# Gathering rows of x and normalising them in place while the table of h is made (24 of 131 groups), with h kept transposed in DRAM and whole blocks of rows to a partition

## The chip, the cores and the metric

The kernel runs on one core of a Trainium2 chip. The metric is the device time of one execution in microseconds (us). The median of three runs of the kernel before is 2666.79 us (2663.8 to 2667.16). The profile and the trace come from another, profiled execution of the same kernel. Lower is better.

## The reference

The kernel computes one layer of a graph network on 12,500 nodes of 256 features, with 200,000 edges sorted by destination:

```python
h = maximum(layernorm(x, axis=-1), 0)
agg = segment_sum(h[src], dst, num_segments=N)
z = (1 + eps_gin) * h + agg
t = relu(batchnorm(z @ W1 + b1, g1, bt1))           # 256 -> 512, statistics over the nodes
out = x + relu(batchnorm(t @ W2 + b2 + h, g2, bt2)) # 512 -> 256
```

All is float32. The index `src` is random, so `h[src]` is a gather of 200,000 rows of 1 KB; each batchnorm needs all nodes before the next step can begin.

## The kernel before

**Indices.** The edges are cut into 1563 tiles of 128 edges, and 12 tiles make a group: 131 groups. src and dst are brought into `srcT` and `dstT`, one column a tile. A `flag` tells whether the destinations are spread evenly enough for the fast form; a branch on it (If and Else, at the end of the program's text) chooses `fast()` or `general()`. Here it is `fast()`.

**The table (lines 257 to 295).** For each of 25 chunks of 512 nodes, rows of x are loaded to `xt`, normalised (per row on DVE BN_STATS and BN_AGGR, square root and the final scaling with relu on ACT), and stored to `h_tab` in DRAM. A partition holds four consecutive rows, so a piece of a transfer is 4 KB (`move`). TensorE transposes the chunk, and DVE and ACT copy it with a stride into `hT`, the transposed h, which stays in SBUF to the end.

**The gather stage (lines 318 to 420).** `gather(i)` issues 12 indirect DMAs on POOL's queue, each of which fetches 128 rows of `h_tab` into a slice of a buffer `gt`. `sums(i)` builds on DVE the 0/1 matrices `oh` (which edge goes to which of 128 local destinations), multiplies them with the gathered rows on TensorE (12 matmuls into one `ps`), copies `ps` to `zs` on ACT, and builds `at`, which places local destinations in a window of 280 nodes. `put(i)` multiplies `zs` with `at` (two matmuls, `pz`) and adds the result to the chunk `zc` on DVE; `zc` begins as hT times 1 + eps on ACT. As soon as a chunk is complete, `first_layer` multiplies it with W1 (16 passes, `ph`), takes statistics on DVE, copies to `ts` on ACT, and stores `t_tab` in DRAM.

A float32 matmul shows as two passes in the profile. The loop issues `gather(i + AHEAD)`, then `sums(i)`, then `put(i - 1)`. With AHEAD = 2 there are three buffers `gt`, so a gather waits until TensorE is done with the group three before. The order of the instructions on each engine is made by a scheduler from the program's text; each engine works through its own list in order, and waits by semaphores: a row that waits holds all that stand behind it.

**Second layer and last pass (lines 425 to 474).** For each chunk `ti` is loaded from t_tab, scaled with relu on ACT (`tT`), multiplied with W2 (`py`), and hT is added in place. After the second statistics, ACT makes `yr` (reading hT with a stride), TensorE transposes back (`po`), DVE adds rows of x (`xr`), and `out` is stored from ACT's queue.

Of the kernel before, what the change touches and what calls it, by code (L numbers as in the profile page):

```python
# [19 lines left out]
AHEAD = 2  # L20
# [8 lines left out]
def kernel(  # L29
# [24 lines left out]
    assert N % R == 0  # L54
# [208 lines left out]
    def fast():  # L263
        with ExitStack() as fs:
            keep = fs.enter_context(tc.tile_pool(name="keep", bufs=1))
            t_tab = dram.tile([NCH, P, HC, CH], F32, name="t_tab")

            hT = [keep.tile([P, DC, w * R], F32, name=f"hT{g}") for g, (_, w) in enumerate(chunks)]


            with tc.tile_pool(name="ln", bufs=3) as ln, tc.tile_pool(
                name="ps_h", bufs=2, space=PSUM
            ) as ps_h:
                for g in range(NCH):
                    n0, w = chunks[g]
                    n = w * R
                    xt = ln.tile([P, R, D], F32, name="xt", bufs=4)
                    move(nc.sync, xt, x, g, store=False)
                    ht = ln.tile([P, R, D], F32, name="ht")
                    layernorm(ln, xt, w, ht)  # L280
                    move(nc.sync, ht, h_tab, g, store=True)
                    pz = ps_h.tile([P, DC, CH], F32, name="pz")
                    for d in range(DC):
                        for c in range(R):
                            nc.tensor.transpose(  # L285
                                pz[:, d, c * w : (c + 1) * w], ht[:w, c, d * P : (d + 1) * P],
                                ident[:w, :w],
                            )
                        side = hT[g][:, d, :].rearrange("p (w c) -> p c w", c=R)
                        came = pz[:, d, :n].rearrange("p (c w) -> p c w", c=R)  # L290
                        if d % 2:
                            nc.scalar.copy(side, came)
                        else:
                            nc.vector.tensor_copy(side, came)


            with ExitStack() as es:
                gat = es.enter_context(tc.tile_pool(name="gat", bufs=AHEAD + 1))
                sel = es.enter_context(tc.tile_pool(name="sel", bufs=2))
                zcp = es.enter_context(tc.tile_pool(name="zc", bufs=3))  # L300
                tsp = es.enter_context(tc.tile_pool(name="ts", bufs=2))
                ps_i = es.enter_context(tc.tile_pool(name="ps_i", bufs=1, space=PSUM))
                ps_s = es.enter_context(tc.tile_pool(name="ps_s", bufs=2, space=PSUM))
                ps_z = es.enter_context(tc.tile_pool(name="ps_z", bufs=1, space=PSUM))
                ps_t = es.enter_context(tc.tile_pool(name="ps_t2", bufs=3, space=PSUM))
# [12 lines left out]

                groups = [(t0, min(GT, NTILE - t0)) for t0 in range(0, NTILE, GT)]
                gathered = {}  # L320

                def gather(i):
                    t0, n = groups[i]
                    gs = []
                    ga = gat.tile([P, GT, D], F32, name="gt")
                    for t in reversed(range(t0, t0 + n)):
                        rows = left if t == full_tiles else P
                        nc.gpsimd.indirect_dma_start(  # L328
                            out=ga[:rows, t - t0, :], out_offset=None, in_=h_tab,
                            in_offset=bass.IndirectOffsetOnAxis(ap=srcT[:rows, t : t + 1], axis=0),  # L330
                        )
                        gs.append((t - t0, rows))
                    gathered[i] = ga, gs
# [3 lines left out]
                def z_chunk(c):  # L337
# [4 lines left out]
                    nc.scalar.activation(zc[c][:, :, :n], hT[c], AF.Copy, scale=gin1)  # L342
# [4 lines left out]
                summed = {}  # L347

                def sums(i):
# [9 lines left out]
                    ga, gs = gathered.pop(i)  # L359
                    ps = ps_s.tile([P, D], F32, name="ps")  # L360
                    for k, (j, rows) in enumerate(gs):
# [362 lines left out]
```

## Time and profile before

| | us |
|---|---|
| median of 3 runs | 2666.79 |
| the profiled execution | 2652.91 |
| its span, first to last instruction | 2651.0 |
| indices, up to the branch | 0 to about 29 |
| table of h | about 29 to 149 |
| gather stage, first to last gather on POOL | 149.1 to 2362.3 |
| its last sums and first layers | 2362 to 2392 |
| second layer | 2392 to 2564 |
| last pass | 2564 to 2651 |

The page names an instruction by line, engine, operation and tiles (out<-in). The engines are PE (TensorE; PEld is its weight load), DVE (VectorE), ACT (ScalarE), POOL (GpSimd) and SP (DMA queues only). In a row of groups stands the busy time, the mean of one in ns, then the idle time of the engine just before and what ended it ("issue": nothing that the profile shows). In a row of waits stands the sum, how often, and the longest. In a timeline a bracket holds the idle time before a row. PEclk is the granted clock of TensorE, 1.00 being full.

### The profile page before, as it was taken

How to read it: one execution, taken by the hardware profiler on the slowest of the kernel's cores; microseconds unless marked ns; L12 is line 12 of the kernel's file. 1: busy time of each engine (PE TensorE's matmuls, PEld its weight loads, DVE VectorE, ACT ScalarE, POOL GpSimd, SP SyncE). 2: the span in 40 equal slices, each digit the busy share in tenths (PEclk: the TensorE clock that was granted, in tenths of full speed). 3: DMA queues.
4: the chain of work that ended last, by engine and by line, in shares of the span. 5: the costliest groups of instructions: out<-in, count | busy, mean ns of one | idle time of the engine just before them, and what ended most of it. 6: DMA issues, size and time to landing. Idle time of an engine off the chain costs nothing.

```text
span 2651.0 us, 14241 instructions
## 1 busy us (share of the span) xinstructions
PE 1623.6 (61%) x4881; PEld 1029.4 (39%) x4881; DVE 633.8 (24%) x1017; ACT 346.8 (13%) x561; POOL 1483.4 (56%) x1575
## 2 busy tenths in 40 slices
PE   3564556755665576556456556666565656569985
PEld 2333344433443343334334334434343334444444
DVE  6611121211221122112112112121121212124443
ACT  4710000000000000000000000000000000004446
POOL 0056667666766666666676676666666676640000
PEclk6566677776776786767777766767776677779985
DMA  5633333333333333333333333333333333325437
GB/s 176 227 101 90 95 101 115 105 95 101 115 105 95 111 105 105 96 111 105 107 97 109 106 98 102 110 105 112 95 105 110 91 114 102 111 78 214 159 130 281
DMA packets 101342, 310.96 MB, mean 117 GB/s; under 512 B 27684, under 2 KB 32362, under 8 KB 95118
## 3 DMA queue, kind: packets, MB, share of 16 engines
q0 software_dynamic: 75008, 204.90, 26.3%
q1 hardware_dynamic: 21744, 91.21, 9.6%
q10 hardware_dynamic: 4510, 13.86, 1.3%
q8 instruction: 41, 0.67, 0.1%
q14 instruction: 39, 0.32, 0.0%
HBM read 258.66 MB, written 51.20 MB: 117 GB/s over the span
## 4 chain that ended last, share of the span: by engine, by line
issue 28%; PE 26%; POOL 25%; another core or an unknown queue 9%; DMA 3%; DVE 2%; ACT 2%; ACTq 0%; POOLq 0%
POOL gt L328 25%; PE ps L362 13%; PE py L441 6%; PE ph L397 4%; DMA gt<-h_tab,srcT 3%; PE pz L380 2%; ACT yr L460 2%; DVE oh L353 1%; PE po L467 1%; DVE zc L389 1%; DVE ot L471 0%; DVE mv L229 0%; DVE at L369 0%; DVE st L401 0%
## 5 line engine op out<-in xcount | busy, mean ns | idle before, releaser
L328 POOL DMA_INDIRECT gt<-h_tab,srcT x1563 | 1481.8, 948 | 850.5 <-issue 458.2
L362 PE MATMUL ps<-gt,oh 128*128 128x256 f32 x3126 | 987.1, 447 | 643.0 <-issue 559.4
L362 PEld LDWEIGHTS ps<-gt,oh 128*128 128x128 f32 x3126 | 672.5, 221 | 949.5 <-issue 738.8
L389 DVE TENSOR_TENSOR zc<-pz,zc 128x560 f32<-128x560 f32 (+9 forms) x203 | 101.0, 527 | 1518.0 <-PE ps L362 863.5
L380 PE MATMUL pz<-at,zs 128*128 128x280 f32 x524 | 194.5, 498 | 181.4 <-DVE zc L389 114.8
L367 ACT COPY zs<-ps 128x256 f32<-128x256 f32 x131 | 48.9, 373 | 1739.4 <-PE ps L362 1147.3
L397 PE MATMUL ph<-zc,w1s 128*128 128x512 f32 (+1 forms) x400 | 197.0, 648 | 80.4 <-DVE zc L389 56.9
L353 DVE TENSOR_TENSOR oh<-col,dstT 128x1536 f32<-128x1536 f32 x131 | 227.8, 1739 | 14.5 <-issue 14.5
L380 PEld LDWEIGHTS pz<-at,zs 128*128 128x128 f32 x524 | 119.5, 237 | 235.0 <-issue 209.2
L441 PE MATMUL py<-tT,w2s 128*128 128x512 f32 (+1 forms) x400 | 169.5, 587 | 4.6 <-ACT tT L434 4.6
L397 PEld LDWEIGHTS ph<-zc,w1s 128*128 128x128 f32 x400 | 82.4, 211 | 181.1 <-issue 117.5
L401 DVE BATCH_NORM_STATS2 st<-ph 128x6 f32<-128x512 f32 (+1 forms) x100 | 68.4, 684 | 265.9 <-remote 93.7
L441 PEld LDWEIGHTS py<-tT,w2s 128*128 128x128 f32 x400 | 76.4, 192 | 97.7 <-issue 86.7
L402 ACT COPY ts<-ph 128x512 f32<-128x512 f32 (+1 forms) x100 | 57.3, 573 | 334.0 <-DVE st L401 251.9
L285 PE MATMUL pz<-ident,ht 128*128 128x128 f32 (+1 forms) x200 | 65.0, 442 | 54.1 <-ACT ht L259 19.5
L434 ACT ACTIVATE tT<-ti,of,sc 128x512 f32<-128x512 f32 (+1 forms) x100 | 72.3, 796 | 91.3 <-issue 86.4
L467 PE MATMUL po<-ident,yr 128*128 128x128 f32 (+1 forms) x200 | 47.6, 413 | 35.6 <-ACT yr L460 35.6
L285 PEld LDWEIGHTS pz<-ident,ht 128*128 128x128 f32 (+1 forms) x200 | 36.6, 205 | 82.5 <-ACT ht L259 40.7
L369 DVE TENSOR_SCALAR at<-col,shift 128x280 f32<-128x280 f32 x131 | 65.5, 500 | 0.0
L460 ACT ACTIVATE yr<-hT,of,sc 128x512 f32<-128x512 f32 (+1 forms) x50 | 59.9, 1276 | 20.1 <-DVE ot L471 19.2
L445 DVE TENSOR_TENSOR hT<-py,hT 128x512 f32<-128x512 f32 (+1 forms) x50 | 33.9, 678 | 100.9 <-PE py L441 100.9
L467 PEld LDWEIGHTS po<-ident,yr 128*128 128x128 f32 (+1 forms) x200 | 37.5, 214 | 45.7 <-ACT yr L460 45.7
(68 smaller groups left out, 307.6 us busy)
## 6 DMA issues: line engine op xcount, KB each, us to landing
gt<-h_tab,srcT POOLq DMA_INDIRECT x1563
t_tab<-ts SPq DMA_DIRECT2D x24, 1024.0 KB
ti<-t_tab SPq DMA_DIRECT2D x24, 1024.0 KB
xt<-in_x_dram SPq DMA_DIRECT2D x24, 512.0 KB
h_tab<-ht SPq DMA_DIRECT2D x24, 512.0 KB
xr<-in_x_dram SPq DMA_DIRECT2D x24, 512.0 KB
out_dram<-ot ACTq DMA_DIRECT2D x24, 512.0 KB
rawi_d<-in_dst_dram SPq DMA_DIRECT2D x1, 768.0 KB
```

What stands on the lines that cost most here:

```text
L285: nc.tensor.transpose(pz[:, d, c * w : (c + 1) * w], ht[:w, c, d * P : (d + 1) * P], ident[:w, :w],)
L328: nc.gpsimd.indirect_dma_start(out=ga[:rows, t - t0, :], out_offset=None, in_=h_tab, in_offset=bass.IndirectOffsetOnAxis(ap=srcT[:rows, t ...
L353: nc.vector.tensor_tensor(oh[:, :n, :], col[:, :P].unsqueeze(1).to_broadcast([P, n, P]), dstT[:, t0 : t0 + n].unsqueeze(2).to_broadcast([P ...
L362: nc.tensor.matmul(ps, lhsT=oh[:rows, j, :], rhs=ga[:rows, j, :], start=(k == 0), stop=(k == n - 1),)
L380: nc.tensor.matmul(pz[:, d, :WIDE], lhsT=zs[:, d * P : (d + 1) * P], rhs=at, start=True, stop=True)
L389: nc.vector.tensor_add(side, pz[:, :, a - lo : b - lo], side)
L397: nc.tensor.matmul(ph[:, :n], lhsT=w1s[:, d, f * P : (f + 1) * P], rhs=zc[c][:, d, :n], start=(d == 0), stop=(d == DC - 1),)
L401: nc.vector.bn_stats(st1[:, f, c, :], ph[:, :n])
L434: nc.scalar.activation(tT[:, f, :n], ti[:, f, :n], AF.Relu, bias=of1[:, f : f + 1], scale=sc1[:, f : f + 1],)
L441: nc.tensor.matmul(py[:, :n], lhsT=w2s[:, f, d * P : (d + 1) * P], rhs=tT[:, f, :n], start=(f == 0), stop=(f == HC - 1),)
L460: nc.scalar.activation(yr[:, d, :, :w], hT[g][:, d, :].rearrange("p (w c) -> p c w", c=R), AF.Relu, bias=of2[:, d : d + 1], scale=sc2[:, d ...
L467: nc.tensor.transpose(po[:w, c, d * P : (d + 1) * P], yr[:, d, c, :w], ident)
```

## The change

- **First groups.** `LEAD` = 24: groups 0 to 23 gather from x itself, not from h_tab. `settle` then normalises the gathered rows in place: six BN_STATS on DVE, each over two rows at once (read alternately, so that the operation's statistics of even and odd elements are those of the two rows), a square root on ACT, two small operations on DVE, and 12 scalings with relu on ACT.
- **The table between them.** There is no table stage. `h_chunk` makes the same 25 chunks within iterations 0 to 19 of the loop: rows normalised by `settle`, stored to h_tab from ACT's queue, transposed through one PSUM bank `pc` (half a chunk at a time), copied to `hc` by DVE or ACT without a stride, and stored to `h_cols`, a new tensor in DRAM that holds h transposed. From group 24 on, gathers read h_tab and wait for its stores.
- **h from DRAM.** `z_chunk` loads zc from h_cols, one chunk ahead, and scales it in place; the second layer loads `yT` from h_cols, after `ti`, and works on it in place of hT.
- **Buffers and order.** AHEAD = 4, so five buffers `gt`; `zc` has four, `ph` two for three. `sums` and `put` are split, so that TensorE's work on `zs` of group i − 1 stands near the beginning of group i's. The 12 matmuls go over the tiles forward, while the gathers are issued backward. t_tab is stored from ACT's queue.
- **Blocks of rows.** `carry` takes the place of `move` in the fast form: partition p takes rows p, 128 + p, 256 + p, 384 + p of a chunk, in pieces of 1 KB. yr is then read and written without a stride, and the last chunk is handled in pieces.
- **Two Ifs** (flag 0, flag 1) for If and Else.

```diff
-AHEAD = 2
+AHEAD = 4
+LEAD = 24
...
+        def carry(eng, sb, table, g, store):
+            n0 = chunks[g][0]
+            for c0, c1, rows in pieces(g):
+                if c0 == c1:
+                    continue
+                side = table[n0 + c0 * P : n0 + (c1 - 1) * P + rows, :].rearrange("(c p) d -> p c d", p=rows)
+                if store:
+                    eng.dma_start(side, sb[:rows, c0:c1, :])
+                else:
+                    eng.dma_start(sb[:rows, c0:c1, :], side)
...
+                def settle(v, pairs, rows, to, tag):
+                    n = 2 * pairs
+                    st = sel.tile([P, n, 3], F32, name="st" + tag)
+                    for c in reversed(range(0, n, 2)):
+                        nc.vector.bn_stats(
+                            st[:, c : c + 2, :].rearrange("p c s -> p (c s)"),
+                            v[:, c : c + 2, :].rearrange("p c d -> p d c"),
+                        )
+                    sd = sel.tile([P, n], F32, name="sd" + tag)
+                    nc.scalar.activation(sd, st[:, :, 2], AF.Sqrt, bias=epst, scale=1.0 / D)
+                    rs = sel.tile([P, n], F32, name="rs" + tag)
+                    nc.vector.reciprocal(rs, sd)
+                    nb = sel.tile([P, n], F32, name="nb" + tag)
+                    nc.vector.scalar_tensor_tensor(nb, st[:, :, 1], -1.0, rs, op0=OP.mult, op1=OP.mult)
+                    for c in reversed(range(rows)):
+                        nc.scalar.activation(
+                            to[:, c, :], v[:, c, :], AF.Relu, bias=nb[:, c : c + 1], scale=rs[:, c : c + 1]
+                        )
...
+                def h_chunk(g):
+                    n = chunks[g][1] * R
+                    slots = len(parts[g])
+                    x_chunk(g + 2)
+                    ht = ln.tile([P, R, D], F32, name="ht")
+                    settle(xts.pop(g), -(-slots // 2), slots, ht, "c")
+                    carry(nc.scalar, ht, h_tab, g, store=True)
+                    hc = ln.tile([P, DC, CH], F32, name="hc")
+                    for d in range(DC):
+                        ph = ps_h.tile([P, CH], F32, name="pc")
+                        for c in range(slots):
+                            nc.tensor.transpose(
+                                ph[:, c * P : (c + 1) * P], ht[:, c, d * P : (d + 1) * P], ident
+                            )
+                        if d % 2:
+                            nc.scalar.copy(hc[:, d, :n], ph[:, :n])
+                        else:
+                            nc.vector.tensor_copy(hc[:, d, :n], ph[:, :n])
+                    nc.sync.dma_start(h_cols[g, :, :, :n], hc[:, :, :n])
...
-                            out=ga[:rows, t - t0, :], out_offset=None, in_=h_tab,
+                            out=ga[:rows, t - t0, :], out_offset=None, in_=x if i < LEAD else h_tab,
...
-                    nc.scalar.activation(zc[c][:, :, :n], hT[c], AF.Copy, scale=gin1)
+                    nc.sync.dma_start(zc[c][:, :, :n], h_cols[c, :, :, :n])
+                    nc.scalar.activation(zc[c][:, :, :n], zc[c][:, :, :n], AF.Copy, scale=gin1)
...
                 for i in range(NG + 1):
+                    while made < NCH and made < 2 + NCH * i // (LEAD - AHEAD):
+                        h_chunk(made)
+                        made += 1
                     if i + AHEAD < NG:
                         gather(i + AHEAD)
+                    pz = None
+                    if i > 0:
+                        join(i - 1)
+                        pz = put(i - 1)
                     if i < NG:
+                        if i < LEAD:
+                            settle(gathered[i], GT // 2, GT, gathered[i], "g")
                         sums(i)
                     if i == 0:
                         continue
-                    put(i - 1)
+                    add(i - 1, pz)
...
                     nc.sync.dma_start(ti[:, :, :n], t_tab[g, :, :, :n])
+                    nc.sync.dma_start(yT[g], h_cols[g, :, :, :n])
...
-    with tc.If(off == 0) as cmp:
+    with tc.If(off == 0):
         fast()
-    with cmp.Else():
+    with tc.If(off == 1):
         general()
```

How the scheduler places this is seen in the lists of the engines. First DVE before, at the end of the table stage (after a chunk's statistics `st` and `mv`; `col` is the constant that the first gather waits for):

```order
L248 BN_STATS st<-xt 53x6
L249 BN_AGGR mv<-st 53x2 [waits DVE_49] x2
L253 RECIPROCAL rs<-sd 53x4 [waits Activation_49]
L294 COPY hT_231<-pz 128x4x128 [waits PE_49]
L255 SCALAR_TENSOR_TENSOR nb<-mv,rs 53x4 [waits DVE_49]
L294 COPY hT_232<-pz 128x4x53 [waits PE_49]
L310 CAST col<-col_i 128x280 [waits Activation_49]
L353 TENSOR_TENSOR oh<-col,dstT 128x1536 [waits DVE_49]
```

And DVE in the change, from the branch on (`stc` are statistics of a chunk, `stg` of gathered rows; DMASW are semaphores of gathers, DMAHW of other transfers):

```order
L767 COMPARE_AND_BRANCH
L109 TENSOR_TENSOR dstT<-dstT,base 128x1572
L313 CAST col<-col_i 128x280 [waits Pool_49]
L317 CAST row<-row_i 128x1 [waits Pool_49]
L407 TENSOR_TENSOR oh<-col,dstT 128x1536 [waits DVE_49]
L320 TENSOR_SCALAR shift<-shift,row 128x131 [waits DVE_49]
L328 BN_STATS stc<-xt 128x6 [waits DMAHW7_49]
```

col stood behind the whole table's work and a wait for ACT; now it stands behind one operation after the branch and waits for POOL alone.

The second place is DVE in the change, some 20 rows on, where the small operations that end the normalising of a group (`rsg`, `nbg`) stand:

```order
L328 BN_STATS stg<-gt 128x6 [waits DMASW3_49,DMASW2_49]
L371 COPY hc<-pc 128x512 [waits PE_49]
L328 BN_STATS stg<-gt 128x6 [waits DMASW5_49,DMASW4_49]
L335 RECIPROCAL rsg<-sdg 128x12 [waits Activation_49]
L335 RECIPROCAL rsc<-sdc 128x4 [waits Activation_49]
L328 BN_STATS stg<-gt 128x6 [waits DMASW7_49,DMASW6_49]
L337 SCALAR_TENSOR_TENSOR nbg<-stg,rsg 128x12 [waits DVE_49]
L337 SCALAR_TENSOR_TENSOR nbc<-stc,rsc 128x4 [waits DVE_49]
L407 TENSOR_TENSOR oh<-col,dstT 128x1536
```

The first rsg belongs to group 0; ahead of it stand the six statistics of group 0, the six of group 1 and one of group 2, each waiting for its own two gathers.

The third place is PE in the middle of the gather stage. Before, around a group's matmuls (`ps`) with those of `put` (`pz`):

```order
L362 MATMUL ps<-gt,oh 128x256 [waits DMASW7_49]
L380 MATMUL pz_2291<-at,zs 128x280 [waits DVE_49,PE_49,Activation_49]
L380 MATMUL pz_2291<-at,zs 128x280
L362 MATMUL ps<-gt,oh 128x256 [waits DMASW0_49,DVE_49]
L362 MATMUL ps<-gt,oh 128x256 [waits DMASW1_49]
L362 MATMUL ps<-gt,oh 128x256 [waits DMASW2_49]
```

In this kernel each of a group's 12 matmuls waits for its own gather, in the order in which the gathers are issued. In the change, after group 24:

```order
L417 MATMUL ps<-gt,oh 128x256 [waits DMASW7_49,DVE_49]
L417 MATMUL ps<-gt,oh 128x256 [waits DMASW6_49]
L436 MATMUL pz_4923<-at,zs 128x280 [waits DVE_49,Activation_49]
L436 MATMUL pz_4923<-at,zs 128x280
L417 MATMUL ps<-gt,oh 128x256 [waits DMASW5_49]
L417 MATMUL ps<-gt,oh 128x256 [waits DMASW4_49]
L417 MATMUL ps<-gt,oh 128x256 [waits DMASW3_49]
L417 MATMUL ps<-gt,oh 128x256 [waits DMASW2_49]
L417 MATMUL ps<-gt,oh 128x256 [waits DMASW1_49]
L417 MATMUL ps<-gt,oh 128x256 [waits DMASW0_49]
L417 MATMUL ps<-gt,oh 128x256 x4
```

The first matmul of a group now waits for the gather that is issued last, and the last four wait for nothing; put's two stand third and fourth. In the first 24 groups a group's 12 matmuls have one wait:

```order
L365 MATMUL pc<-ident,ht 128x128 [waits PE_49,Activation_49]
L365 MATMUL pc<-ident,ht 128x128 x3
L436 MATMUL pz_1300<-at,zs 128x280 [waits Activation_49]
L436 MATMUL pz_1300<-at,zs 128x280
L365 MATMUL pc<-ident,ht 128x128 [waits DVE_49]
L365 MATMUL pc<-ident,ht 128x128 x3
L417 MATMUL ps<-gt,oh 128x256 [waits Activation_49]
L417 MATMUL ps<-gt,oh 128x256 x11
```

The transposes of the table's chunks (`pc`, two times four) stand between, each half waiting for the copy that empties the one PSUM bank, and the sums wait for ACT's scaling of the rows.

More of the change, by code (lines that the diff above doesn't have):

```diff
@@ L264, in fast @@
         with ExitStack() as fs:
             keep = fs.enter_context(tc.tile_pool(name="keep", bufs=1))
+            h_cols = dram.tile([NCH, P, DC, CH], F32, name="h_cols")
             t_tab = dram.tile([NCH, P, HC, CH], F32, name="t_tab")
[L268 to L294, printed above, removed]
@@ L422, in fast @@
             sc1, of1 = norm(keep, st1, mv1, HC, g1c, bt1c, b1c, "1")
+            late = fs.enter_context(tc.tile_pool(name="late", bufs=1))
+            yT = [late.tile([P, DC, w * R], F32, name=f"yT{g}") for g, (_, w) in enumerate(chunks)]
             with tc.tile_pool(name="tin", bufs=4) as tin, tc.tile_pool(name="tsb", bufs=2) as tsb, tc.tile_pool(
```

84 lines of the change are left out of this document (55 added, 29 removed).

## The prediction

> **What bounds the kernel now.** I read the page's slices first, for the stages, then the windows, POOL's waits, and the timeline at its pauses.
>
> ```profile
> span 2651.0 us, 14241 instructions
> ...
> POOL 0056667666766666666676676666666676640000
> ```
>
> The row shows POOL in 40 slices of 66 us. POOL, which issues the gathers, is idle for two slices (the table of h is made) and for the last four (second layer, last pass); in between it is at six tenths, and no engine is full. The windows give the stages (columns: PE, PEld, DVE, ACT, POOL busy, granted clock, DMA share, GB/s):
>
> ```profile
> 30.00:150.00 120.00, 65.01 (x200) 36.58 (x200) 74.74 (x281) 84.16 (x154) 0.94 (x2) 0.50 0.60 214
> 150.00:2350.00 2200.00, 1311.53 (x3982) 859.94 (x3982) 430.20 (x548) 123.68 (x242) 1471.42 (x1553) 0.73 0.34 104
> 2392.00:2564.00 172.00, 169.48 (x400) 76.41 (x400) 70.17 (x106) 71.81 (x100) 0.00 (x0) 0.99 0.44 156
> 2564.00:2651.00 87.00, 47.62 (x200) 37.49 (x200) 30.97 (x28) 59.86 (x50) 0.00 (x0) 0.57 0.72 260
> ```
>
> So 2200 of 2651 us are the gather stage. What POOL waits for there:
>
> ```profile
> POOL gt L328 <- issue: 458.2, 1501, 0.6
> POOL gt L328 <- PE ps L362: 194.0, 42, 9.6
> POOL gt L328 <- DVE col L310: 119.1, 1, 119.1
> POOL gt L328 <- remote: 78.7, 17, 6.6
> L328 POOL DMA_INDIRECT gt<-h_tab,srcT x1563 | 1481.8, 948 | 850.5 <-issue 458.2 <-PE ps L362 194.0 <-DVE col L310 119.1
> ```
>
> A gather takes 0.948 us and 458.2/1501 = 0.305 us to the next, so 1.253 us, 15.04 us for a group of 12. The single wait of 119.1 us is the table stage. The other 272.7 us are pauses at the heads of groups, until PE has freed a buffer. The timeline of POOL at some restarts (the pause in brackets):
>
> ```profile
> 149.12 1.10 POOL L328 DMA_INDIRECT gt<-h_tab,srcT  x1 [119.06 <-DVE col L310]
> ...
> 233.69 0.95 POOL L328 DMA_INDIRECT gt<-h_tab,srcT  x1 [9.56 <-PE ps L362]
> ...
> 966.36 0.95 POOL L328 DMA_INDIRECT gt<-h_tab,srcT  x1 [4.32 <-remote]
> ...
> 1017.26 0.94 POOL L328 DMA_INDIRECT gt<-h_tab,srcT  x1 [6.11 <-PE ps L362]
> ...
> 1051.32 0.95 POOL L328 DMA_INDIRECT gt<-h_tab,srcT  x1 [4.31 <-remote]
> ...
> 1834.96 0.95 POOL L328 DMA_INDIRECT gt<-h_tab,srcT  x1 [6.15 <-PE ps L362]
> ...
> 1867.60 0.94 POOL L328 DMA_INDIRECT gt<-h_tab,srcT  x1 [2.88 <-remote]
> ...
> 1886.07 0.95 POOL L328 DMA_INDIRECT gt<-h_tab,srcT  x1 [3.73 <-remote]
> ```
>
> Between restarts less pause, divided by 15.04, lie 5 groups (84.57 us), 3 (50.90), 2 (34.06), 2 (32.64) and 1 (18.47). The pause grows with the groups issued since the last one: 9.6 after five, 6.1 after three, 4.3 after two; where one came early (2.88 after two) the next is longer (3.73 after one) and the two together are again 51.11 us for three. Something is worked off at **17.03 us a group** whatever the pauses do, and POOL runs ahead of it by 2 us a group. PE shows the same from the other side:
>
> ```profile
> 1007.11 0.59 PE L362 MATMUL ps<-gt,oh 128*128 128x256 f32 x1 [2.22 <-issue]
> 1009.91 0.58 PE L362 MATMUL ps<-gt,oh 128*128 128x256 f32 x1 [2.21 <-issue]
> ...
> 1014.81 3.32 PE L362 MATMUL ps<-gt,oh 128*128 128x256 f32 x5 [1.52 <-issue]
> ```
>
> While POOL issues, a pass starts every 2.80 us with nothing named as waited for; in POOL's pause before 1017.26 five run in 3.32 us. What is worked off the trace does not say. That buffers only shift pauses, I conclude from the pairs above.
>
> **The change part by part.** *Start.* Gathers no longer wait behind the table: DVE's col is now written right after the branch, where the row of dstT stands today:
>
> ```profile
> 29.30 1.79 DVE L108 TENSOR_TENSOR dstT<-dstT,base 128x1572 f32<-128x1572 f32 x1 [0.75 <-DVE flag L205]
> ```
>
> The first gather then comes at about 30: **−119.1 us**, the whole of the wait.
>
> *Groups 0 to 23.* 24 groups now share their time with the normalising of their own rows and with 25 table chunks, made in 20 iterations (1.25 a group). Prices:
>
> ```profile
> L362 PE MATMUL ps<-gt,oh 128*128 128x256 f32 x3124 | 986.5, 447 | 643.0 <-issue 559.4 <-DMA gt<-h_tab,srcT 67.8 <-DVE oh L353 7.1
> L380 PE MATMUL pz<-at,zs 128*128 128x280 f32 x524 | 194.5, 498 | 181.4 <-DVE zc L389 114.8 <-issue 52.0 <-remote 14.5
> L397 PE MATMUL ph<-zc,w1s 128*128 128x512 f32 (+1 forms) x400 | 197.0, 648 | 80.4 <-DVE zc L389 56.9
> L285 PE MATMUL pz<-ident,ht 128*128 128x128 f32 x192 | 63.2, 447 | 52.3 <-ACT ht L259 18.4 <-DVE mv L249 11.7 <-DVE st L248 9.4
> L259 ACT ACTIVATE ht<-xt,nb,rs 128x256 f32<-128x256 f32 x96 | 50.6, 593 | 13.6 <-issue 6.2 <-ACT sd L251 4.3 <-DVE rs L253 2.6
> L251 ACT ACTIVATE sd<-mv,epst 128x4 f32<-128x4 f32 x24 | 6.6, 288 | 3.8 <-DVE nb L255 3.3 <-DVE mv L249 0.5
> L402 ACT COPY ts<-ph 128x512 f32<-128x512 f32 x96 | 55.9, 583 | 327.8 <-DVE st L401 245.8 <-issue 56.9 <-DVE oh L353 25.1
> L367 ACT COPY zs<-ps 128x256 f32<-128x256 f32 x131 | 48.9, 373 | 1739.4 <-PE ps L362 1147.3 <-remote 469.0 <-issue 82.3
> L401 DVE BATCH_NORM_STATS2 st<-ph 128x6 f32<-128x512 f32 x96 | 67.0, 698 | 264.9 <-remote 93.7 <-PE ps L362 66.2 <-issue 60.3
> L353 DVE TENSOR_TENSOR oh<-col,dstT 128x1536 f32<-128x1536 f32 x130 | 227.3, 1748 | 14.5 <-issue 14.5
> L294 DVE COPY hT<-pz 128x512 f32<-128x512 f32 x24 | 25.5, 1062 | 24.5 <-PE pz L285 24.5
> L166 DVE COPY dstT<-pt 128x512 f32<-128x512 f32 x3 | 2.1, 692 | 0.8 <-PE pt L164 0.8
> ```
>
> ACT, a group: 12 × 0.593 on the gathered rows, 0.29 and 0.37, 1.25 × (4 × 0.593 + 0.29 + 0.58) for the chunk, 4 × 0.58 × 25/131 of first layer: 12.3 us, and zc below a half more. DVE: 6 bn_stats of 512 elements, from 0.70 (contiguous) to 0.70 × 1062/692 = 1.07 (a strided copy against a contiguous one), 4.2 to 6.4; 1.25 × (2 of them and a copy of 0.69) = 2.6 to 3.5; oh 1.75; below 2.5 for the small ones: 11 to 14 us. Both are under 17.03. PE: 24 × 0.447 + 4 × 0.498 + 197.0/131 = 14.2 us as before, and 10 transposes of 0.447: **18.7 us** at the traced means. These hold slow passes, so the group costs from 15.04 (POOL alone, if PE catches up) to 18.7; I take 18.0, near the upper end, since the added passes go through the engine that POOL already waits for. 24 × (18.0 − 17.03) = **+23 us** (−48 to +40). The cover for this work is that buffers are five: in the order on DVE the small operations that end group i's normalising stand behind bn_stats that wait for a later group's rows, which uses up about two of the five.
>
> *The clock in these groups.* PE now waits for one signal from ACT and then has 12 matmuls at once. In the table stage, where it works in pieces, the granted clock is 0.50, in the second layer 0.99. At the half clock a pass of 256 costs 0.46 (the last flush, 4.60 us for ten):
>
> ```profile
> 2366.87 4.60 PE L362 MATMUL ps<-gt,oh 128*128 128x256 f32 x10 [0.82 <-issue]
> 2371.30 1.11 PE L380 MATMUL pz<-at,zs 128*128 128x280 f32 x4
> 2373.51 7.03 PE L397 MATMUL ph<-zc,w1s 128*128 128x512 f32 x16
> ```
>
> 24 × 0.46, 4 × 0.56 (twice 1.11/4), 10 × 0.447 and 2 × 7.03 × 25/131 give 20.4 us a group: 24 × (20.4 − 18.0) = +58 us on the sum. The Trainium skill ("TensorE: Matmul & The Clock Gate", "HAM oscillation — how this bites in real kernels") says that PE falls back to the half clock after some 3.4 us without work, every time; by that rule this is the case. The gather stage's 0.73, with its waits of 2 us and pauses of its own, agrees only in part.
>
> *The seam.* The first gather from h_tab (group 24) waits for all stores of the table; the last chunk is made four iterations earlier, about four groups of 17 us. Between 0 and 17 us, I take +3, since SP and ACT's queues have nothing else by then.
>
> *Groups 24 to 130.* 107 groups × 17.03 = 1822, as before; PE's matmuls now wait for a group's last gather first, which five buffers cover: **0**. Between 107 × (15.04 − 17.03) = −213, if buffers do absorb the pauses, and 0. I take 0 by the conserved 51 us. The store of t_tab moves to ACT, whose 124 of 2200 us leave room.
>
> *h in DRAM.* 12.8 MB written and read twice beside a DMA share of 0.34: hidden. In the second layer five loads of yT (2.6 MB) stand on SP ahead of the first ti; at 260 GB/s, the last stage's, that is 10 us. Before, ti loads started under the gather stage's end; yT must wait for the space of its buffers. **+10 us** (0 to 15). Later, 1.57 MB a chunk in 6.9 us is 229 GB/s, under 260.
>
> *Last pass.* ACT reads yr without the stride (59.86 us less about a third), but rows now move in pieces of 1 KB, not 4 KB:
>
> ```profile
> q0 software_dynamic: 75008, 204.90, 26.3%
> q1 hardware_dynamic: 21744, 91.21, 9.6%
> ```
>
> q0 (the gathers, 1 KB rows) moves 204.90 MB in 26.3% of 2651 us, 294 GB/s while busy; q1 358. A DMA share of 0.72 becomes 0.72 × 358/294 = 0.88 of the same 87 us. Between 87 × (0.88 − 1) = −10 and +9 for a ramp like that of the busy share lost now; I take 0. *Two Ifs* for one If with Else: a second branch at the end, which costs DVE 0.75 us at the first (above); between 0 and 3, I take +1.
>
> Sum: 2651.0 − 119.1 + 23 + 3 + 10 + 1 = 2569 us of span. The profiled execution took 2652.91, 1.9 above its span, and the median of the runs is 2666.79, 13.9 more: **2585 us**.
>
> **The rivals.** *Buffers absorb the pauses.* For it: POOL alone could do 1.253 us, and PE's dense passes show it has room. Against: the conserved 17.03. First gather at 30, 1563 × 1.253 = 1958, then the 288.7 us that lie behind the last issue now, and 11: 2288, as a median **2304**; half of the pauses gone is some 2445.
>
> *The first groups go serial (slower).* ACT's stream holds, between the 12 rows' activations, copies of the transposes that wait for PE, and PE's matmuls wait for ACT. With PE's results late as in the rows at 1007, neither runs under the other: 12 × 0.593 + 18.7 = 25.8 us a group, 24 × (25.8 − 17.03) = +210, 2651.0 − 119.1 + 210 + 14 = 2756, as a median **2772**. It decides from 17.03 + (119.1 − 14)/24 = 21.4 us a group on. Against: five buffers, and slack of about one group.
>
> *Half clock throughout the first groups:* 2585 + 58 = **2643**.
>
> *The change doesn't do it:* something in the first gather's wait still stands behind the table's work, and all stays but the +14: about 2680. Only DVE's order speaks on it, and there col is ahead.
>
> **How the numbers follow.** Forecast 0.52 (own range 2535 to 2625), buffers absorb 0.17 (2304 to 2535), half clock 0.13 (2625 to 2660), serial 0.14 (2672 to 2772; a few hundredths of it near zero), no effect 0.04. The range of 8 in 10 leaves out the fuller half of the first rival and the upper half of the slower one: 2360 to 2700. What this kernel's measurement can tell from no change is about 0.2%, 5 us: faster 0.52 + 0.17 + 0.12 = 0.81, same 0.04, slower 0.15.
>
> **What would show it.** First gather near 30 us, not 149. Restarts of POOL after group 24 still conserving 17 us a group: then the step on the buffers holds; POOL without pauses would break it. Group 24's first gather at 30 + 24 × 18 = 462, within 15 us; if near 545 or later, the serial rival. A granted clock of 0.5, or one above 0.7, in the windows up to 460. The second layer's first matmul some 10 us later against the last gather than the 30 us of now. The forecast is wrong above all if the 17.03 us hang on the order of PE's waits, which the change turns round, and not on the gathers.

## The result, and the profile after

The changed kernel takes 2589.44 us (median of 4 runs, 2577.98 to 2596.73) against 2666.15 (median of 4, 2663.80 to 2667.16) before: a ratio of 0.971, with an interval of 0.967 to 0.9749. It was forecast at 2585 us. The profiled execution took 2577.98 us, with a span of 2576.2; the stages below are of this one, against the 2651.0 us of before.

The later runs fell on several chips, and for these kernels there are two kinds: the kernel before takes 2655 to 2668 us on the one (below: a chip with the pauses; the result above is from one) and 2387 to 2389 us on the other (a chip without them).

POOL's waits, and its timeline at the first gather, at group 24, at a stretch in the middle, and at the last gather but one:

```profile
POOL gt L382 <- issue: 450.8, 1477, 0.6
POOL gt L382 <- remote: 198.2, 41, 6.4
POOL gt L382 <- ACT zs L424: 72.8, 18, 8.1
POOL col_i L311 <- issue: 29.7, 1, 29.7
POOL gt L382 <- PE ps L417: 25.8, 13, 2.4
```

```profile
32.45 1.61 POOL L382 DMA_INDIRECT gt<-in_x_dram,srcT  x1 [0.42 <-issue]
...
462.67 0.95 POOL L382 DMA_INDIRECT gt<-h_tab,srcT  x1 [3.23 <-ACT sdg L333]
...
1418.78 0.94 POOL L382 DMA_INDIRECT gt<-h_tab,srcT  x1 [6.44 <-remote]
...
1453.33 0.94 POOL L382 DMA_INDIRECT gt<-h_tab,srcT  x1 [4.57 <-remote]
...
1487.45 0.94 POOL L382 DMA_INDIRECT gt<-h_tab,srcT  x1 [4.43 <-remote]
...
2274.52 0.94 POOL L382 DMA_INDIRECT gt<-h_tab,srcT  x1 [0.30 <-issue]
```

The single wait of 119.1 us is gone: the first gather is issued at 32.45 us. The pauses are not. The waits for a "remote" release (a signal came, and the trace doesn't say from whom), ACT and PE shown here come to 297 us, as against 273 before, though there are five buffers for three. Two groups lie between the restarts at 1418.78, 1453.33 and 1487.45, again in 34.1 to 34.6 us with a pause of 4.4 to 4.6.

The windows of the first groups, of the steady part and of the last pass (columns as before):

```profile
32.00:116.00 84.00, 12.67 (x45) 9.59 (x46) 30.85 (x55) 20.23 (x43) 57.57 (x62) 0.54 0.58 181
116.00:462.00 346.00, 211.47 (x758) 154.06 (x757) 178.06 (x338) 197.55 (x418) 215.91 (x228) 0.76 0.62 196
462.00:2275.00 1813.00, 938.39 (x3296) 698.70 (x3297) 371.40 (x472) 126.43 (x245) 1207.07 (x1275) 0.74 0.36 109
2500.00:2576.00 76.00, 40.27 (x196) 37.51 (x196) 30.13 (x26) 35.67 (x50) 0.00 (x0) 0.68 0.89 297
```

In the first groups ACT is busy 57% and DVE 51% of the time; neither is full. In the last pass ACT is down from 59.86 us to 35.67 and the DMA engines are up from 0.72 to 0.89.

Between the gather stage and the second layer, on ACT, SP and PE (timelines):

```profile
2315.70 0.60 ACTq L464 DMA_DIRECT2D t_tab<-ts  x1
```

```profile
2309.69 2.42 SPq L507 DMA_DIRECT2D yT<-h_cols  x5
2319.94 8.45 SPq L506 DMA_DIRECT2D ti<-t_tab  x5
```

```profile
2325.98 4.63 PE L517 MATMUL py<-tT,w2s 128*128 128x512 f32 x5 [11.99 <-ACT tT L510]
```

PE waits 12 us for the first tT, and that waits for the first ti, which SP issues only 4 us after the last t_tab store.

### The profile page after: what moved, and what is told of

It is laid out like the page before. It is cut to its first block, busy times and chain, and to the rows that moved or that the text cites. A ratio compares the mean times of both kernels' runs of the same rounds, so it can differ in the third digit from the quotient of the medians.

```text
span 2576.2 us, 14802 instructions
## 1 busy us (share of the span) xinstructions
PE 1418.7 (55%) x4873; PEld 1010.7 (39%) x4873; DVE 714.3 (28%) x1060; ACT 460.5 (18%) x871; POOL 1482.6 (58%) x1575
## 4 chain that ended last, share of the span: by engine, by line
another core or an unknown queue 49%; PE 29%; ACT 7%; issue 6%; DVE 4%; DMA 3%; SPq 0%; POOL 0%; ACTq 0%; DVEq 0%; POOLq 0%
PE ps L417 12%; PE py L517 7%; PE pz L436 5%; PE ph L458 4%; ACT gt L339 3%; DMA out_dram<-ot 1%; ACT zs L424 1%; ACT ht L339 1%; DVE oh L407 1%; DVE st L462 1%; DMA zc<-h_cols 1%; DVE zc L449 1%; PE pc L365 1%; ACT ts L463 1%
## 5 line engine op out<-in xcount | busy, mean ns | idle before, releaser
L382 POOL DMA_INDIRECT gt<-h_tab,srcT x1275 | 1207.5, 947 | 608.5 <-issue 370.9
L417 PE MATMUL ps<-gt,oh 128*128 128x256 f32 x3126 | 776.9, 409 | 55.5 <-ACT gt L339 42.8
L417 PEld LDWEIGHTS ps<-gt,oh 128*128 128x128 f32 x3126 | 654.2, 210 | 175.3 <-ACT gt L339 46.6
L382 POOL DMA_INDIRECT gt<-in_x_dram,srcT x288 | 273.5, 949 | 154.0 <-issue 79.9
L458 PE MATMUL ph<-zc,w1s 128*128 128x512 f32 (+1 forms) x400 | 218.2, 699 | 252.2 <-ACT ts L463 231.9
L339 ACT ACTIVATE gt<-gt,nbg,rsg 128x256 f32<-128x256 f32 x288 | 149.5, 590 | 4.0 <-DVE nbg L337 1.9
L328 DVE BATCH_NORM_STATS2 stg<-gt 128x6 f32<-128x512 f32 x144 | 91.4, 689 | 34.2 <-DMA gt<-in_x_dram,srcT 31.2
L521 DVE TENSOR_TENSOR yT<-py,yT 128x512 f32<-128x512 f32 (+1 forms) x50 | 33.9, 679 | 110.5 <-PE py L517 108.5
L365 PE MATMUL pc<-ident,ht 128*128 128x128 f32 x196 | 39.2, 334 | 40.6 <-DVE hc L371 16.8
L542 PE MATMUL po<-ident,yr 128*128 128x128 f32 x196 | 40.3, 394 | 33.5 <-ACT yr L536 33.5
```

Of the source, the lines that this page charges most:

```text
L328: nc.vector.bn_stats(st[:, c : c + 2, :].rearrange("p c s -> p (c s)"), v[:, c : c + 2, :].rearrange("p c d -> p d c"),)
L339: nc.scalar.activation(to[:, c, :], v[:, c, :], AF.Relu, bias=nb[:, c : c + 1], scale=rs[:, c : c + 1])
L382: nc.gpsimd.indirect_dma_start(out=ga[:rows, t - t0, :], out_offset=None, in_=x if i < LEAD else h_tab, in_offset=bass.IndirectOffsetOnAxi ...
L417: nc.tensor.matmul(ps, lhsT=oh[:rows, j, :], rhs=ga[:rows, j, :], start=(j == 0), stop=(j == n - 1))
L458: nc.tensor.matmul(ph[:, :n], lhsT=w1s[:, d, f * P : (f + 1) * P], rhs=zc[c][:, d, :n], start=(d == 0), stop=(d == DC - 1),)
```

## The experiments

The theory after the result: gathers are worked off at 17.0 us a group of 12, POOL issues them at 15.0, and neither the number of buffers nor the order or amount of PE's work changes that; the gain is the earlier start and no more. Its rivals: buffers absorb pauses; PE's passes, or the order of its waits, make the pace.

### Three buffers

```diff
-AHEAD = 4
+AHEAD = 2
...
-made < 2 + NCH * i // (LEAD - AHEAD)
+made < 2 + NCH * i // (LEAD - 4)
```

> The change with AHEAD = 2 (three gather buffers for five), the table's chunks still made in 20 iterations. Theory (gathers are worked off at about 17 us a group whatever the buffers): from group 24 on the restarts of POOL still lie 17.0 us a group apart, and after the last gather about 12 us are saved, since PE is two groups behind instead of four (in the change the last four groups take it 6.1 us each). In the first 24 groups three buffers don't cover the normalising, which ends two groups after the landing: 22 to 26 us a group for 17.9. Sum 2589 - 12 + 24 x (4 to 8) = 2675 to 2770 us. Rival (the deeper buffers are what absorbs pauses): steady pace worse than 17.3 us a group.

> As before, the change with three gather buffers, in the hope of a place where the kernel before takes 2666 us. There: theory (17.0 us a group whatever the buffers): 17.0 us a group from group 24 on, 2675 to 2770 us by the first groups at 22 to 26 us each; where the kernel before takes 2387 us, 2344 again. Rival (deeper buffers absorb pauses): steady pace over 17.3 us a group.

The first run (2344.27 us, median of 4) fell on a chip where the kernel before takes 2387.32; the second (2587.71, one run) on one where it takes 2655.28. On the chip without the pauses POOL stops in the first 24 groups alone, and never later; the unaltered change never stops and takes 2274.53 on another such chip (below). So five buffers are worth 70 us there, all in the first groups: group 24 comes at 462.90 us, in the change at 392.69. On the chip with the pauses group 24 comes at 492.22 us, 30 us later than in the change, or 19.2 us a group, and what follows goes on at 17.0 us a group:

```profile
492.22 0.94 POOL L382 DMA_INDIRECT gt<-h_tab,srcT  x1 [4.79 <-ACT zs L424]
```

Its total lies within the range of the change's runs. My 22 to 26 us a group were too much. As I read it, a pause that comes from the normalising also lets the backlog run off, so that it replaces a pause instead of adding to it; no run isolates that.

### Without the overlap

```diff
                 x_chunk(0)
                 x_chunk(1)
+                for g in range(NCH):
+                    h_chunk(g)
...
-in_=x if i < LEAD else h_tab
+in_=h_tab
...
-                        if i < LEAD:
-                            settle(gathered[i], GT // 2, GT, gathered[i], "g")
```

> The change without its overlap: all 25 chunks of the table are made first, then all 131 groups gather from h_tab and none is normalised in place; five buffers, h in DRAM, the rows by blocks, the order of matmuls and the two Ifs stay. Theory (the gain is the start alone): first gather near 149 us less what the new table code saves, 17.0 us a group from there to the end, so 2589 + (149 - 32) - 24 x (17.93 - 17.03) = 2684 us, 2660 to 2690. Rival (the rest of the change saves time by itself, by the buffers or the last pass): under 2640.

It took 2408.87 us where the kernel before takes 2387.32, a ratio of 1.0094 (1.0077 to 1.0111). POOL's waits:

```profile
POOL gt L382 <- issue: 470.9, 1546, 0.3
POOL gt L382 <- DMA h_cols<-hc: 139.7, 1, 139.7
```

The wait for the table is 139.7 us, 20.6 longer than in the profile of before (which is from a chip with the pauses), and the total is 21.6 us longer. So everything in the change but the overlap costs about 20 us, probably since a chunk's two halves go through one PSUM bank one after the other and 12.8 MB more are written. The overlap alone is worth 2408.87 − 2274.53 = 134 us on chips of this kind (the two runs are from two of them), which is about the wait that it hides. And there is no pause at all among 1563 gathers: the 17.0 us are not a property of the kernel. My 2660 to 2690 us were meant for a chip with the pauses, where this kernel was not run.

### One matmul of twelve

```diff
-                    for j in range(n):
+                    for j in range(1):
```

The sums of the other 11 tiles are left out.

> The change with one matmul of 12 in a group (the sums of the other 11 tiles are left out), so PE's work in the stage falls from 24 + 4 + 3 passes a group to 2 + 4 + 3. Theory (what is worked off hangs on the gathers, not on PE's passes): POOL still pauses, 17.0 us a group from group 24 on, last gather near 2275 us, and the total is 2589 - 20 for the groups that PE no longer has to finish at the end. Rival (PE's passes are what limits): the pauses go, 15.04 us a group, 107 x 2 = 213 us less in the steady part and the first groups faster too: 2330 to 2370 us.

> As before, the change with one matmul of 12 in a group (the other 11 tiles' sums are left out), hoping for a place where the kernel before takes 2666 us. There: theory (what is worked off hangs on the gathers, not on PE's passes): POOL still pauses, 17.0 us a group from group 24 on, total 2589 - 20. Rival (PE's passes limit): no pauses, 2266 us as where the kernel before takes 2387 us.

The same kernel took 2266.08 us on a chip of the one kind (before: 2387.32) and 2561.76 on one of the other (2655.28); one run each. The second settles most. PE is busy in only 143 of the 500 us from 1000 to 1500 us, and POOL still pauses; POOL's restart after 120 gathers in a row:

```profile
1278.40 0.95 POOL L382 DMA_INDIRECT gt<-h_tab,srcT  x1 [18.21 <-remote]
```

Ten groups, 18.2 us: 1.8 us a group, as it was 9.56 after five and 6.1 after three. From restart to restart (group 29 at 571.34 us, group 125 at 2187.62) it is 16.84 us a group. The timelines of PE and ACT at the end of this burst show where the time sits:

```profile
1235.39 3.78 PE L458 MATMUL ph<-zc,w1s 128*128 128x512 f32 x4 [6.35 <-issue]
1245.70 2.24 PE L436 MATMUL pz<-at,zs 128*128 128x280 f32 x4 [6.53 <-issue]
1252.20 3.78 PE L458 MATMUL ph<-zc,w1s 128*128 128x512 f32 x4 [4.26 <-issue]
1255.77 1.06 PE L417 MATMUL ps<-gt,oh 128*128 128x256 f32 x2
1278.65 2.23 PE L436 MATMUL pz<-at,zs 128*128 128x280 f32 x4 [21.82 <-ACT zs L424]
```

```profile
1234.75 0.59 ACT L463 COPY ts<-ph 128x512 f32<-128x512 f32 x1 [22.06 <-issue]
1245.28 0.37 ACT L424 COPY zs<-ps 128x256 f32<-128x256 f32 x1 [9.93 <-remote]
1251.56 0.59 ACT L463 COPY ts<-ph 128x512 f32<-128x512 f32 x1 [5.91 <-DVE st L462]
...
1278.22 0.37 ACT L424 COPY zs<-ps 128x256 f32<-128x256 f32 x1 [14.88 <-remote]
```

PE is idle for many us between a few passes. For three of these waits the profile names nothing ("issue"), but each of them ends within 0.1 us of the end of a copy on ACT (1235.34, 1245.65, 1252.15): PE waits for ACT, and ACT for PE. The matmul ps ends at 1256.8, and its copy begins at 1278.22, 21 us later; the pz that needs the copy, and POOL, go on right then. From 1263.4 to 1271.8 no engine works, and the DMA share is 0.00, so that neither work nor a transfer is waited for. PE's results reach the other engines late. It is so before POOL stops, too: while POOL still issues a group in 15.0 us, these copies come 16.80 us apart (and the next, behind passes of first_layer, only at 1245.28).

```profile
1178.72 0.37 ACT L424 COPY zs<-ps 128x256 f32<-128x256 f32 x1 [15.03 <-remote]
1195.52 0.37 ACT L424 COPY zs<-ps 128x256 f32<-128x256 f32 x1 [16.43 <-issue]
1212.32 0.37 ACT L424 COPY zs<-ps 128x256 f32<-128x256 f32 x1 [16.43 <-remote]
```

On the chip without pauses, the same group of instructions waits for one thing only, the gathers (window 600 to 1900):

```profile
L417 PE MATMUL ps<-gt,oh 128*128 128x256 f32 x174 | 106.0, 713 | 822.1 <-DMA gt<-h_tab,srcT 822.1
```

So PE's amount of work is not what is worked off, and the rival falls. The total on the chip with pauses is 2561.76, near the 2569 that the theory gave.

### The matmuls in the order of the gathers

```diff
-                    for j in range(n):
+                    for j in reversed(range(n)):
...
-start=(j == 0), stop=(j == n - 1)
+start=(j == n - 1), stop=(j == 0)
```

> The change with each group's 12 matmuls again in the order of its gathers, so that PE can follow the gathers one by one. Theory (rate fixed per gather): 17.0 us a group in the steady part, total within 10 us of the change's 2589. Rival (the pace hangs on the order of PE's waits): a steady pace that differs by over 0.3 us a group, over 32 us in all.

It took 2264.46 us where the kernel before takes 2387.32 (0.9489, 0.9474 to 0.9505), so the question about the pace could not be answered there. It is answered by the next kernel, which has this order too and ran where POOL pauses.

### yT behind ti

```diff
                     nc.sync.dma_start(ti[:, :, :n], t_tab[g, :, :, :n])
-                    nc.sync.dma_start(yT[g], h_cols[g, :, :, :n])
+                    nc.gpsimd.tensor_copy(yT[g][:, 0, :1], ti[:, 0, :1])
+                    nc.gpsimd.dma_start(yT[g], h_cols[g, :, :, :n])
```

with the matmuls in the order of the gathers.

> The change with matmuls in the order of the gathers, and with the loads of yT on POOL's queue behind a copy of one column of the chunk's ti, so that they can't stand ahead of the first ti. Theory (the 12 us that PE waits for ti at the start of the second layer are the five yT loads on SP): PE's wait there falls from 12 us to under 4, 8 to 10 us less than the change with the matmuls alone put back (2264 us where the kernel before takes 2387). Rival (the loads only move, and the second layer waits for yT instead): within 3 us of it.

> The change itself, unaltered, beside the kernel before on the same chip. In the runs so far the kernel before took 2666 us in one place and 2387 us in another, and there POOL made no pauses at all in the steady part. Theory (the pace of 17.0 us a group is a state of the chip and no property of the kernel): where the kernel before takes about 2387 us, the change has POOL at 15.0 us a group throughout, first gather at 32, last at about 1990, then some 278 us: 2265 to 2285 us, ratio 0.95 to 0.957; where it takes about 2666, 2589 us again, ratio 0.971. Rival (the kernel's order brought the pauses, by chance of a run): a change that pauses although the kernel before does not.

Both on one chip where the kernel before takes 2668.19: the unaltered change 2582.41 (0.9684, 0.9641 to 0.9726), this one 2584.81 (0.9708, 0.9644 to 0.9771). The pace after the first groups is 17.1 us a group in both, so the order of PE's waits doesn't make it. And PE still waits; SP, then PE:

```profile
2324.49 8.21 SPq L506 DMA_DIRECT2D ti<-t_tab  x5
```

```profile
2330.26 5.19 PE L518 MATMUL py<-tT,w2s 128*128 128x512 f32 x7 [10.72 <-ACT tT L511]
```

The last store of t_tab, on ACT:

```profile
2321.25 0.60 ACTq L464 DMA_DIRECT2D t_tab<-ts  x1
```

No yT load stands ahead of ti any more, and ti is still issued 3 us after that store. My theory on yT falls. The suspicion that was left: ti is laid where ts was, and must wait until the store has read it.

### The pools in another order

```diff
+                tsp = es.enter_context(tc.tile_pool(name="ts", bufs=2))
                 ln = es.enter_context(tc.tile_pool(name="ln", bufs=2))
-                gat = es.enter_context(tc.tile_pool(name="gat", bufs=AHEAD + 1))
                 sel = es.enter_context(tc.tile_pool(name="sel", bufs=2))
                 zcp = es.enter_context(tc.tile_pool(name="zc", bufs=4))
-                tsp = es.enter_context(tc.tile_pool(name="ts", bufs=2))
+                gat = es.enter_context(tc.tile_pool(name="gat", bufs=AHEAD + 1))
```

> The change with one thing altered: the order in which the gather stage's pools are laid out in SBUF, ts first and the gather buffers last, so that the second layer's ti takes the space of the gather buffers instead of that of ts. Theory (the 12 us wait of PE at the start of the second layer is ti's wait for the last store out of ts, whose space it takes, and not the five yT loads on SP): the first ti loads are issued before the last first_layer, PE's wait before py falls from 12 us to under 3, about 10 us less. Rival (it is bandwidth, or the statistics' chain): PE's wait stays over 8 us.

The ti loads now come before the last store of ts, and PE waits 3.7 us for 12 (SP, ACT, PE):

```profile
2341.56 3.41 SPq L506 DMA_DIRECT2D ti<-t_tab  x4
```

```profile
2349.29 0.60 ACTq L464 DMA_DIRECT2D t_tab<-ts  x1
```

```profile
2351.28 8.96 PE L517 MATMUL py<-tT,w2s 128*128 128x512 f32 x14 [3.71 <-ACT tT L510]
```

The yT loads come behind ti here too (at 2357.69), but so they did in the run before, where PE still waited 10.7 us; what is new is the space. The cause is shown, though the wait is not under 3 us as I had said. The total, 2600.90 us where the kernel before takes 2655.28 (0.9795, 0.9752 to 0.9838), is not better than the change's: in this execution the first groups held pauses of 15 to 20 us and the last gather was issued 36 us later. Whether the layout does that or chance, this run alone doesn't tell; in the next pair the same layout has no such pauses, but on a chip without the pauses, so this stays open.

### The change and the best version side by side

The best version has both edits, the order of the matmuls and that of the pools.

> The change unaltered again, as the partner of the next kernel on the same chip. Where the kernel before takes 2650 to 2670 us: 2575 to 2600, steady pace 17.0 to 17.1 us a group, PE's wait before the second layer 12 us. Where it takes about 2387: 2265 to 2285 us and no pauses after group 24.

> The change with both edits that may help: matmuls in the order of the gathers, and the pools laid out so that ti takes the gather buffers' space. Theory: PE's wait before the second layer falls from 12 to under 4 us, the order of the matmuls does nothing, so 8 us less than the unaltered change on the same chip, within the 10 us by which runs differ where POOL pauses, and clearly where it doesn't. Rival (the layout or the order slows the gather stage, as the 1 us a group more in the first groups of the run with the pools alone might mean): no faster than the unaltered change.

Both on one chip where the kernel before takes 2389.24 us: the change 2274.53 (0.9521, 0.9505 to 0.9537), the best version 2258.49 (0.9457, 0.9441 to 0.9473). In the change there, POOL and PE look as they should:

```profile
POOL gt L382 <- issue: 466.7, 1532, 0.4
POOL col_i L311 <- issue: 29.3, 1, 29.3
POOL gt L382 <- DMA gt<-h_tab,srcT: 2.1, 7, 0.3
```

```profile
L417 PE MATMUL ps<-gt,oh 128*128 128x256 f32 x3124 | 863.5, 435 | 623.3 <-DMA gt<-h_tab,srcT 583.5 <-ACT gt L339 39.8
```

No pause is left, and PE waits for gathers. The first gather is issued at 32.06 and the last ends at 1985.73, 1563 × 1.25 us. PE's last first_layer and its first py, of the change and then of the best version:

```profile
2004.50 3.92 PE L458 MATMUL ph<-zc,w1s 128*128 128x212 f32 x16 [0.45 <-DVE zc L449]
2020.30 10.07 PE L517 MATMUL py<-tT,w2s 128*128 128x512 f32 x19 [11.88 <-ACT tT L510]
```

```profile
1996.94 3.92 PE L458 MATMUL ph<-zc,w1s 128*128 128x212 f32 x16 [0.45 <-DVE zc L449]
2004.56 15.92 PE L517 MATMUL py<-tT,w2s 128*128 128x512 f32 x30 [3.70 <-ACT tT L510]
```

Of the 16 us between the two, PE's wait before py gives 8, and the order of the matmuls the other half, which I had put at nothing: the last first_layer begins 7.6 us earlier, since PE has followed the last gathers one by one. The kernel with that order alone has it at 1997.98, 6.5 us earlier than the change.

### Half the rows

```diff
-                        rows = left if t == full_tiles else P
+                        rows = left if t == full_tiles else P if i < LEAD else P // 2
```

the same in the matmuls. Half of the edges from group 24 on are left out.

> The change with gathers of 64 rows for 128 from group 24 on (the other half of those edges is left out); the number of gathers stays. It asks what the pace of 17.0 us a group is charged by. Theory A (by the gather: its instruction, its semaphores): POOL, faster by itself with 64 rows, is held to 17.0 us a group by longer pauses. Theory B (by the row or byte): 8.5 us a group or POOL's own pace, whichever is longer, so the pauses go or shrink in proportion. Where the kernel before takes 2387 us no pauses are expected by either, and the run only gives POOL's own time for 64 rows.

It fell where there are no pauses, so what the pace is charged by was not found out. It gives POOL's own time:

```profile
L382 POOL DMA_INDIRECT gt<-h_tab,srcT x1275 | 1149.4, 901 | 388.5 <-issue 371.2 <-PE ps L417 16.4 <-DVE zc L449 0.3
```

0.901 us for 64 rows against 0.945 for 128 on the same chip: a gather costs POOL nearly the same with half the rows.

## Why the prediction was right, and which of its steps were not

The sum was 2569 us of span, and the span is 2576.2. By its steps, between the profiled executions:

| step | forecast | measured | from |
|---|---|---|---|
| first gather | −119.1 | −116.7 | 149.12 to 32.45 |
| groups 0 to 23, and the seam | +23, +3 | +21.8 | 430.2 us to group 24's first gather, 408.5 before |
| groups 24 to 130 | 0 | +8 | 17.07 us a group, 16.99 before |
| last gather to first py | +10 | +20.8 | 50.5 us, 29.7 before |
| second layer | 0 | +1.4 | 173.9 us to the first yr, 172.5 before |
| last pass | 0 | −10.2 | 76.3 us, 86.5 before |
| Ifs | +1 | not seen | |

**The start and the pace held.** Group 24's first gather was forecast at 462 us and came at 462.67. (The 16.99 of the table runs from group 24's first gather to group 130's; the 17.03 of the prediction, from restart to restart.) The step that buffers only move pauses was argued from five pairs of restarts; three buffers where POOL pauses, and a kernel with a twelfth of the matmuls there, now show it. That it is "worked off whatever the pauses do" was right for the chips of that kind and wrong as a property of the kernel: on the other kind the pauses after the first groups don't exist, and the rival *buffers absorb the pauses*, which I had put at 2304 us, describes POOL there almost exactly (2274.53 us in all), though not by the buffers: the kernel with three has no steady pauses either.

**The first groups** cost 17.93 us each against the 18.0 taken. The reason that I gave, PE's passes, is not borne out: with a twelfth of the matmuls, on a chip with the pauses, these groups took 18.9 us each (31.83 to 485.22 us), no less. On a chip without the pauses they cost nothing beyond POOL's own pace, 15.03 us each in the change (32.06 to 392.69 us). So the 18.0 was right by luck, and what makes up the 17.93 stays open.

The half clock came in part. The granted clock is 0.54 up to 116 us, where PE has 12.67 us of work in 84. The 0.76 from there to group 24 is a mean of stretches at 0.50 (198.7 to 222.4 us, for one) and at 1.00 (223.0 to 242.9 us), and PE is idle 16 times there for 3.6 to 8.8 us. The rule of the Trainium skill ("TensorE: Matmul & The Clock Gate", "HAM oscillation — how this bites in real kernels") fits both. It is not all: before, the clock was 0.50 from 993 to 1014 us, where PE worked in 4.87 of 21 us but was never idle for more than 2.3. The +58 us did not come with it: I had taken them from PE's passes, and a twelfth of the passes did not make these groups shorter either.

The serial rival (21.4 us a group and more) did not occur on either kind of chip.

**The tail was mis-sized, and its cause was wrong.** I charged 10 us to five yT loads ahead of ti. PE does wait 12.0 us there, where it waited 4.6 before, but the loads are not why: ti takes the space of ts and waits for its last store, as the kernel with the pools in another order shows. The row of before:

```profile
2392.04 1.22 PE L441 MATMUL py<-tT,w2s 128*128 128x512 f32 x1 [4.62 <-ACT tT L434]
```

And I had left out a term: where POOL pauses, PE stands as many groups behind it as there are buffers to fill, four at the last gather for two. PE's last groups in the change:

```profile
2281.92 5.34 PE L417 MATMUL ps<-gt,oh 128*128 128x256 f32 x24
...
2288.04 5.34 PE L417 MATMUL ps<-gt,oh 128*128 128x256 f32 x24
```

A group takes it 6.1 us when nothing holds it; two more are 12.2, and with the 7.4 of the wait that is 19.6 of the 20.8 us. With three buffers, on a chip with the pauses, the step takes 42.7 us, 7.8 less than the change's 50.5, although PE waits 14.3 us before py for 12.0; so 10 of the 12.2 us go with the buffers.

**The last pass** I put at nothing, between −10 and +9. It came out at −10.2: the DMA share rose to 0.89 as worked out, but at 297/0.89 = 334 GB/s while busy, not at the 294 of the gathers' pieces (before: 260/0.72 = 361), and ACT's activations fell from 1297 to 803 ns, so that, as I read it, less was lost between transfers:

```profile
L536 ACT ACTIVATE yr<-yT,of,sc 128x512 f32<-128x512 f32 x48 | 34.8, 803 | 31.7 <-DVE ot L548 30.8 <-DVE of L241 0.9
```

The tail's error (+10.8 us) and this one (−10.2 us) cancel; that the total lies within 5 us of the forecast owes something to that, and to the chip: on one without the pauses the change takes 2274.53 us, far below the range that I gave.

## What to carry to other kernels

When a wait has the same length per unit of work however the pauses fall, look for something that is worked off at a fixed rate, and don't expect buffers to help; what starts the stream earlier still helps in full. A wait at the seam of two stages can come from where a buffer lies: before a queue's order is blamed, see which store the new tile's space has to wait for. And time a kernel beside the old one on the same chip, since the same program differed by 12% between chips here, and a change was worth 3% on the one and 5% on the other.

## What the runs showed of the hardware that was not expected

The kernel before takes 2655 to 2668 us on some chips and 2387 to 2389 us on others, with POOL's own time for a gather the same (0.948 and 0.945 us). The difference, 266 to 281 us, is about the 272.7 us of pauses in the profile of before; none of the seven kernels run on a chip without them pauses after group 24. Where the pauses occur, PE's results are seen by ACT, DVE and POOL up to 21 us late while POOL issues indirect gathers, and PE starts passes after idle times for which the profile names no wait; some time after POOL stops (18 us above), that ends. The backlog grows by 1.8 to 2.0 us for 12 gathers, hardly by PE's work, the number of buffers or the order of PE's waits. What it consists of stays open: the run that would have told whether it goes by the gather or by the row fell on a chip without it. So does why only some chips have it; each chip of the later runs was seen in one session, so that it may also be a passing state.

One thing goes with it. No profile from a chip with the pauses gives a time from issue to landing for the gathers, and every profile from the others does. The row of the page, for the change on the one kind and on the other:

```profile
gt<-h_tab,srcT POOLq DMA_INDIRECT x1275
```

```profile
gt<-h_tab,srcT POOLq DMA_INDIRECT x1275, 2.8
```

The record of the signals is thus not complete where POOL pauses: "issue" and "remote" there do not show that nothing, or something outside the core, was waited for. Whether the recording itself has a part in the pauses, no run here tests.
